# Moving the Mamba layer's x branch from the second phase of a four-layer kernel to the first, with its end states by DMA and two of sixteen states scaled by diagonals

## The chip, the cores and the metric

The kernel runs on one core of one Trainium2 chip. The metric is the device time of one execution in microseconds. The kernel before takes 10303.82 us, the median of 3 runs (10300.73 to 10316.85).

## The reference, cut to what matters

Eight samples of 256 channels on a 32 x 32 image go through four layers: a block of attention and feed-forward, a second attention block, a quantized convolution block, and a Mamba layer that scans the image in four orders (rows, rows backwards, columns, columns backwards). The change concerns the last:

```python
def _selective_scan(u, dt, A, Bm, Cm):
    def step(h, inp):
        u_t, dt_t, B_t, C_t = inp
        dA = jnp.exp(dt_t[:, :, None] * A)
        h = h * dA + dt_t[:, :, None] * B_t[:, None, :] * u_t[:, :, None]
        y = jnp.einsum('bdn,bn->bd', h, C_t)
        return (h, y)
...
def _mamba(u, W_in, conv_w, conv_b, W_x, W_dt, b_dt, A_log, D, W_out):
    xz = u @ W_in.T
    x, z = jnp.split(xz, 2, axis=-1)
    xc = x.swapaxes(1, 2)
    xc = jax.lax.conv_general_dilated(xc, conv_w[:, None, :], (1,), [(D_CONV - 1, 0)], feature_group_count=D_INNER) + conv_b[None, :, None]
    x = jax.nn.silu(xc).swapaxes(1, 2)
    x_dbl = x @ W_x.T
    dt = jax.nn.softplus(x_dbl[..., :DT_RANK] @ W_dt.T + b_dt)
    Bm = x_dbl[..., DT_RANK:DT_RANK + D_STATE]
    Cm = x_dbl[..., DT_RANK + D_STATE:]
    A = -jnp.exp(A_log)
    y = _selective_scan(x, dt, A, Bm, Cm) + x * D
    y = y * jax.nn.silu(z)
    return y @ W_out.T
```

There are 512 inner channels (4 chunks of 128 partitions), 16 states, and 1024 tokens in a sequence. The four orders of a sample share the projection x; the convolution over 4 tokens looks back in its own direction, so it differs for each.

## The kernel before, in words

Every operation is first described as an object (`_Op`, L113) with an estimated cost and the 512-column blocks that it reads and writes. Strands (Python generators) yield such operations. A planner (`_Order`, L171) always emits the strand's operation that could start first by its estimates, ties by rank; what it emits is the fixed program order of each engine, and the SP queue too is issued in that order. Since all operations leave through one helper (L136), nearly every row of the profile has line L136, and rows are told apart by tile names. Buffers come from rooms (`_Room`): a strand that takes from an empty room waits until another has put a buffer back.

**Phase A** (`phase_a`, L265) does layers 0 to 2 for all eight samples, some three of them in flight. Attention goes over TensorE (scores and values in tile `bank`), VectorE (maxima, `stats`) and ScalarE (exponentials, `exps`). Depthwise taps use ScalarE and GpSimd (`outer_taps`, L669) or VectorE (`feed_forward`, L784). Where the planner foresees a gap on TensorE it puts filler products (`fill`, L1059; their row has L1081). `layer2` (L994) ends by writing 8-bit codes to DRAM twice, as they are and turned to column order by a GpSimd copy (`codes[b][0]`, `codes[b][1]`). `weight_parts` (L1108) splits W_in into three bf16 parts and keeps them in DRAM (`w_in`). Weights stay in SBUF from the start.

**Phase B** (`phase_b`, L1142) does the Mamba layer as 64 blocks: 8 samples x 2 token orders (`swap`) x 2 directions (`back`) x 2 halves of 512 tokens. Each block has 16 groups, one for each state. What a block needs is prepared one or two blocks ahead by strands that `ahead` (L1592) starts at fixed groups:

- `inputs` (L1242): for each sample and order, x from codes and `w_in` by six bf16 products for each of 4 chunks x 2 halves, evicted by VectorE into `xi`.
- `mixed` (L1267): `conv` makes three of the four taps as fp32 products with diagonals `cvd` on TensorE and the fourth by VectorE into `xs`; `xdbl` projects `xs` to `xd`, stores the C rows to DRAM (`c_d`) and transposes B to `bT`.
- `steps` (L1315): dt from `xd` (`dt`), dt times x on GpSimd (`tmp`), transposed on TensorE and copied by VectorE to `du`, tokens on partitions.
- `tables` (L1356): one batch on ScalarE of silu of `xs` (and of the gate `z` in a quarter of the blocks) and softplus of `dt`, then back to the table with exp and ln: three table loads.

Then a group s runs over four engines. `scales` (L1453): ScalarE multiplies the four token tiles of `du` by B's column s, 128x512 each, into `dbu`. `turns` (L1463): TensorE transposes these, 16 of 128x128, into `db` in PSUM. `decays` (L1481): ScalarE makes exp(dt A) for each chunk, `da`. `scans` (L1500): VectorE's scan over `da` and `db` for each chunk, two chunks to a pair `h`. `ends` (L1522): in a block that is the first half of its direction, a ScalarE copy keeps each pair's last column in `st`, the start value for the other half. `products` (L1534): GpSimd multiplies the pair in place by C's row, which SP spreads from DRAM to all partitions (`rows`, L1493, `cb`). `sums` (L1543): TensorE transposes and adds the pair into four accumulators `py`; at group 1 x times D is added; at the end the four `py` go to `yT`, and `fold` and `outputs` finish.

The rooms that set how far an engine may run ahead are 5 `da`, 12 `dbu`, 3 `db` banks, 6 pairs `h`, 3 `cb`.

Of the kernel before, what the change touches and what calls it, by code (L numbers as in the profile page):

```python
# [42 lines left out]
TH = HALF // P  # L43
PAD = 3
# [30 lines left out]
def tile_conv_seq(ctx: ExitStack, tc: tile.TileContext, i: dict, out: bass.AP):  # L75
# [7 lines left out]
    def col(name, k=0, n=1):  # L83
# [6 lines left out]
    codes = [  # L90
        [dram.tile([CC, P, N], BF16, name=f"codes{b}_{k}", tag=f"codes{b}_{k}") for k in range(2)] for b in range(B)
# [4 lines left out]
    phase_a(tc, i, col, ident, codes, parts)  # L96
    phase_b(tc, i, col, ident, codes, parts, out)


class _Op:  # L100


    def __init__(self, engine, method, args, kw):
# [12 lines left out]
        elif engine == "vector":  # L116
            fast = near and method in ("tensor_scalar", "tensor_copy")
            both = near and method == "tensor_tensor"
            scan = method == "tensor_tensor_scan"
            self.cost = 0.04 + n * (2.2 if scan else 0.57 if fast else 1.1) + (0.3 if fast or both else 0)  # L120
        elif engine == "scalar":
            self.cost = 0.05 + 0.87 * n + (0.13 if len(ins) > 1 else 0)
        elif engine == "gpsimd":
            self.cost = 0.17 + 2.17 * n if method == "tensor_tensor" else 0.3 + n
        else:
            self.cost, self.landing = 0.1, 3.0

    @staticmethod
    def blocks(a):
        step = max(1, a.ap[0][0])  # L130
        lo = a.offset % step
        hi = lo + sum((n - 1) * abs(s) for s, n in list(a.ap)[1:])
        return [(a.name, k) for k in range(lo // 512, hi // 512 + 1)]
# [131 lines left out]
def phase_a(ctx, tc, i, col, ident, codes, w_parts):  # L265
# [19 lines left out]
    NBIG, NMID, NLOW = 12, 9, 7  # L285
# [7 lines left out]
    exps = _Room(rooms, "exps", 4, [P, 2, HALF])  # L293
    stats = _Room(rooms, "stats", 3, [P, 2, 2, NT, 4])
    bank = _Room(banks, "bank", 8, [P, HALF])
    take, takes, put = order.take, order.takes, order.put

# [3 lines left out]
    w_pi = ldk("w_pi", CC, 2 * HID)  # L301
# [3 lines left out]
    w_qkv1 = ldk("w_qkv1", CC, 3 * C)  # L305
# [478 lines left out]
    def feed_forward(b, x):  # L784
# [10 lines left out]
        at, ready, active, finished = [0], [0], [0], [0]  # L795

        def chunk(o):
            yield lambda: at[0] == o and active[0] < 2
            active[0] += 1
            at[0] += 1  # L800
            hx = yield from take(mid)
            for h in range(2):
                ps = yield from side()
                yield mm(ps, w_pi, o * P, (o + 1) * P, xn, h)
                yield A.copy(hx[:, hs(h)], ps)
                back(ps)
            acc = yield from take(mid)
# [92 lines left out]
    def layer1(b, x):  # L900
# [7 lines left out]
        ready = [0, 0]  # L908
        for cc in range(CC):
            for n, dst in enumerate((q, k)):  # L910
                for h in range(2):
                    ps = yield from side()
                    yield mm(ps, w_qkv1, n * C + cc * P, n * C + (cc + 1) * P, xn, h)
# [4 lines left out]
                    back(ps)  # L918

# [4 lines left out]
        for cc in range(CC):  # L924
            for h in range(2):
                ps = yield from side()
                yield mm(ps, w_qkv1, 2 * C + cc * P, 2 * C + (cc + 1) * P, xn, h)
                yield A.copy(v[:, cc, hs(h)], ps)
                back(ps)
        put(big, xn)  # L930
# [63 lines left out]
    def layer2(b, x):  # L994
# [34 lines left out]
        for cc in range(CC):  # L1029
# [14 lines left out]
            turned = yield from take(low, [P, N], BF16)  # L1044
            yield G.tensor_copy(turned.rearrange("p (b a) -> p b a", a=HH), cd.rearrange("p (a b) -> p b a", b=WW))
            for k, t in enumerate((cd, turned)):
                yield S.dma_start(codes[b][k][cc], t)
                put(low, t)
# [39 lines left out]
    def sample(b):  # L1088
# [17 lines left out]
        stage[b] = 4  # L1106

    def weight_parts():  # L1108


        for m, to in enumerate(w_parts):
# [9 lines left out]
            put(low, o)  # L1121

# [19 lines left out]
def phase_b(ctx, tc, i, col, ident, codes, w_parts, out):  # L1142
# [14 lines left out]
    xi_room = _Room(rooms, "xi", DC, [P, N + 2 * PAD])  # L1157
# [5 lines left out]
    h_room = _Room(rooms, "h", 6, [P, 2, HALF])  # L1163
    cb_room = _Room(rooms, "cb", 3, [P, HALF])
    tmp_room = _Room(rooms, "tmp", 2, [P, HALF])
    z_room = _Room(rooms, "z", DC, [P, HALF])
# [25 lines left out]
    cvd = wp.tile([P, DC, 3, P], F32, name="cvd", tag="cvd")  # L1192
    for c in range(DC):
        for k in range(3):
            nc.gpsimd.tensor_scalar(cvd[:, c, k, :], ident, col("cv_w", 4 * c + k), None, ALU.mult)
# [15 lines left out]
    def load_x(b, swap, h, box):  # L1211

        xf = yield from take(xf_room)
        yield S.dma_start(xf, codes[b][swap][:, :, hs(h)].rearrange("k p n -> p k n"))
# [27 lines left out]
    def inputs(b, swap, xi):  # L1242


        def first(h, box):
            if h == 0:
                tiles = yield from takes(DC, xi_room)
                for c, t in enumerate(tiles):
                    yield G.memset(t[:, :PAD], 0.0)
                    yield G.memset(t[:, PAD + N :], 0.0)  # L1250
                    xi[c] = t
            yield from load_x(b, swap, h, box)

        def one(h, c, box):
            room, ps = yield from project(box, c * P)
            yield V.tensor_scalar(xi[c][:, PAD + h * HALF : PAD + (h + 1) * HALF], ps, col("s3"), None, ALU.mult)
            put(room, ps)
            xi["done"] = xi.get("done", 0) + 1

        for h in range(2):  # L1260
            box = []
            yield first(h, box)
            for c in range(DC):
                yield one(h, c, box)


    def mixed(n):  # L1267

        d, h = blocks[n]
        xi, xd = xis[d.b, d.swap], xds[n % 2]  # L1270
        done = d.done[h]

        def conv(c):
            yield lambda: xi.get("done", 0) == 2 * DC
            t = yield from take(xs_room)
            room, ps = yield from lend()
            for k in range(3):
                o = PAD + h * HALF + (PAD - k if d.back else k - PAD)
                yield T.matmul(
                    ps, lhsT=cvd[:, c, k, :], rhs=xi[c][:, o : o + HALF], start=(k == 0), stop=(k == 2)  # L1280
                )
            o = PAD + h * HALF
            yield V.scalar_tensor_tensor(t, xi[c][:, o : o + HALF], col("cv_w", 4 * c + 3), ps, ALU.mult, ALU.add)
            put(room, ps)
            d.xs[c, h] = t
            done.add(c)
            xi["used"] = xi.get("used", 0) + 1
            if xi["used"] == 4 * DC:
                for k in range(DC):
                    put(xi_room, xi[k])  # L1290

        def xdbl():
            yield lambda: "silu" in done and (n < 2 or "dt" in blocks[n - 2][0].done[blocks[n - 2][1]])
# [19 lines left out]
        return [conv(c) for c in range(DC)] + [xdbl()]  # L1313

    def steps(n):  # L1315
# [6 lines left out]
        def dt(c):  # L1322
# [12 lines left out]
            yield lambda: "soft" in done  # L1335
# [16 lines left out]
    xis = {(b, swap): {} for b in range(B) for swap in (False, True)}  # L1352
# [3 lines left out]
    def tables(n=None, m=None, z=None):  # L1356


        def ready():
            return (  # L1360
                (n is None or len([c for c in range(DC) if c in blocks[n][0].done[blocks[n][1]]]) == DC)
                and (m is None or len(raw[m]) == DC)
                and (z is None or len(gates[z]) == DC)
            )
# [3 lines left out]
        if n is not None:  # L1368
            d, h = blocks[n]
            ops += [A.activation(d.xs[c, h], d.xs[c, h], AF.Silu, bias=col("cv_b", c)) for c in range(DC)]  # L1370
# [385 lines left out]
```

## Time and profile before

| what | us |
|---|---|
| median of 3 runs | 10303.82 |
| the profiled execution | 10303.42 |
| its span | 10301.6 |
| busy: PE / ACT / DVE / POOL | 9415.7 / 8514.4 / 7759.3 / 6131.8 |
| last `codes` store (end of phase A) | 3693 |
| first scan / last scan | 3764 / 10266 |

The page's second part shows the two phases: forty slices of the span, each digit the busy share in tenths.

```profile
PE   9989989999999989989898999899989999989988
PEld 3333323333333347777776777777777777777676
DVE  6367467575667458888887888888888888888788
ACT  7867677867666759988898998989898889899888
POOL 1433032242121048878787787778787778787778
```

The first fourteen slices are phase A, with TensorE nearly full and GpSimd little used; the rest is phase B, with all four engines at 7 to 9 tenths. The costliest rows of the groups read: line, engine, operation, written from read, count, then busy time and mean ns of one, then idle time of the engine just before, and what ended most of it.

```profile
L136 POOL TENSOR_TENSOR h<-h,cb 128x1024 f32<-128x1024 f32 x2048 | 4813.3, 2373 | 1039.1 <-DVE h L136 367.0
L136 ACT ACTIVATE da<-dt,am 128x512 f32<-128x512 f32 x4096 | 2872.0, 714 | 543.2 <-DVE h L136 537.6
L136 ACT ACTIVATE dbu<-du,bT 128x512 f32<-128x512 f32 x4096 | 2798.1, 710 | 15.4 <-PE db L136 13.6
L136 DVE TENSOR_TENSOR_SCAN h<-da,db 128x512 f32<-128x512 f32 x2048 | 2338.9, 1202 | 460.2 <-ACT da L136 131.9
L136 DVE TENSOR_TENSOR_SCAN h<-da,st,db 128x512 f32<-128x512 f32 x2048 | 2465.9, 1262 | 258.8 <-ACT da L136 139.3
L136 PE MATMUL pp<-xi,cvd 128*128 128x512 f32 x1488 | 687.8, 598 | 1.6 <-DVE ys L136 1.6
```

A group's busy time overlaps that of its neighbours, so the parts of an engine add up to more than the engine's busy time; an fp32 product counts as two records, a transpose as one.

### The profile page before, as it was taken

The page shows a single profiled execution, that of the slowest core. Times are in us where ns is not written, and L with a number is a line of the kernel's source. Part 1 is how long each engine was busy: PE and PEld are TensorE (multiplying, and loading weights), DVE is VectorE, ACT ScalarE, POOL GpSimd, SP SyncE. Part 2 cuts the span into 40 slices and gives each one's busy share as a digit, 9 for nine tenths or more (in the row PEclk, how much of TensorE's full clock was granted, in tenths as well). Part 3 has the DMA queues.
Part 4 walks back from the last instruction along what each step waited for, and adds up shares of the span by engine and source line. Part 5 has one row for each costly group of instructions (what it writes and reads, how often), then busy time and mean ns, then how long its engine had stood idle before and what let it go on. Part 6 is the DMA issues. An engine that isn't in the chain of part 4 may idle for free.

```text
span 10301.6 us, 149772 instructions
## 1 busy us (share of the span) xinstructions
PE 9415.7 (91%) x55378; PEld 5953.1 (58%) x55499; DVE 7759.3 (75%) x8675; ACT 8514.4 (83%) x15869; POOL 6131.8 (60%) x2988
## 2 busy tenths in 40 slices
PE   9989989999999989989898999899989999989988
PEld 3333323333333347777776777777777777777676
DVE  6367467575667458888887888888888888888788
ACT  7867677867666759988898998989898889899888
POOL 1433032242121048878787787778787778787778
PEclk7988989989888899999999999999999999999999
DMA  2000000000000011112111112111111111111111
GB/s 58 30 19 17 21 21 19 17 26 17 13 17 9 17 34 51 53 44 59 46 52 53 46 52 59 43 52 56 49 51 48 56 50 49 55 52 46 57 43 52
DMA packets 219616, 415.83 MB, mean 40 GB/s; under 512 B 25137, under 2 KB 67505, under 8 KB 213762
## 3 DMA queue, kind: packets, MB, share of 16 engines
q1 hardware_dynamic: 218882, 406.24, 13.1%
q8 instruction: 437, 7.16, 0.3%
q14 instruction: 297, 2.43, 0.1%
HBM read 358.43 MB, written 37.22 MB: 38 GB/s over the span
## 4 chain that ended last, share of the span: by engine, by line
PE 28%; ACT 22%; DVE 8%; issue 3%; POOL 1%; DMA 1%; DVEq 0%; SPq 0%; POOLq 0%; ACTq 0%
PE pp L136 11%; PE py L136 9%; ACT da L136 9%; PE db L136 8%; ACT dbu L136 8%; DVE h L136 7%; ACT L136 2%; ACT xs L136 1%; ACT dt L136 1%; POOL h L136 1%; ACT L145 1%; DMA wi<-w_in 1%; DVE ys L136 1%; ACT st L136 0%; ACT z L136 0%
## 5 line engine op out<-in xcount | busy, mean ns | idle before, releaser
L136 POOL TENSOR_TENSOR h<-h,cb 128x1024 f32<-128x1024 f32 x2048 | 4813.3, 2373 | 1039.1 <-DVE h L136 367.0
L136 ACT ACTIVATE da<-dt,am 128x512 f32<-128x512 f32 x4096 | 2872.0, 714 | 543.2 <-DVE h L136 537.6
L136 ACT ACTIVATE dbu<-du,bT 128x512 f32<-128x512 f32 x4096 | 2798.1, 710 | 15.4 <-PE db L136 13.6
L136 PE MATMUL db<-ident,dbu 128*128 128x128 f32 x16384 | 2385.7, 280 | 362.2 <-DVE h L136 322.6
L136 DVE TENSOR_TENSOR_SCAN h<-da,db 128x512 f32<-128x512 f32 x2048 | 2338.9, 1202 | 460.2 <-ACT da L136 131.9
L136 DVE TENSOR_TENSOR_SCAN h<-da,st,db 128x512 f32<-128x512 f32 x2048 | 2465.9, 1262 | 258.8 <-ACT da L136 139.3
L136 PEld LDWEIGHTS db<-ident,dbu 128*128 128x128 f32 x16384 | 1885.2, 143 | 875.4 <-DVE h L136 539.6
L136 PE MATMUL py<-ident,h 128*128 128x128 f32 x16384 | 2141.8, 278 | 92.4 <-POOL h L136 75.5
L136 PEld LDWEIGHTS py<-ident,h 128*128 128x128 f32 x16384 | 1878.3, 143 | 227.0 <-POOL h L136 144.2
L136 DVE TENSOR_REDUCE stats<-bank 128x1 f32<-128x512 f32 x1536 | 983.4, 684 | 545.1 <-PE bank L136 544.0
L136 ACT ACTIVATE bank<-bank,stats 128x512 f32<-128x512 f32 x1536 | 1024.9, 672 | 432.1 <-DVE stats L136 424.5
L136 PE MATMUL bank<-big,big 32*128 32x512 f32 x4096 | 987.3, 713 | 37.9 <-ACT bank L136 27.7
L136 POOL TENSOR_TENSOR mid<-mid,mid 128x961 f32<-128x961 f32 (+2 forms) x192 | 397.2, 2076 | 992.9 <-ACT mid L136 663.6
L136 ACT ACTIVATE exps<-bank 128x512 f32<-128x512 f32 x1536 | 796.5, 620 | 165.9 <-PE bank L136 156.6
L136 PE MATMUL pp<-xi,cvd 128*128 128x512 f32 x1488 | 687.8, 598 | 1.6 <-DVE ys L136 1.6
L136 PEld LDWEIGHTS bank<-big,big 32*128 32x128 f32 x4096 | 334.7, 204 | 523.7 <-issue 219.7
L136 DVE SCALAR_TENSOR_TENSOR mid<-mid,cols,mid 128x961 f32<-128x961 f32 (+1 forms) x384 | 601.6, 1567 | 6.3
L136 PE MATMUL bank<-exps,big 128*32 128x512 f32 (+1 forms) x3072 | 547.9, 621 | 3.7 <-ACT exps L136 3.7
L136 PE MATMUL bank<-big 32*128 32x512 f32 x2048 | 517.4, 724 | 32.1 <-ACT bank L136 21.5
L136 POOL TENSOR_TENSOR tmp<-dt,xs 128x512 f32<-128x512 f32 x256 | 320.9, 1273 | 322.0 <-ACT dt L136 224.4
L136 POOL TENSOR_SCALAR big<-big,ga,gs 128x512 f32<-128x512 f32 x64 | 67.7, 1070 | 712.3 <-DVE gs L136 385.5
L136 POOL TENSOR_TENSOR big<-big,mid 128x961 f32<-128x961 f32 (+1 forms) x128 | 315.2, 2472 | 270.7 <-ACT mid L136 268.6
(204 smaller groups left out, 9116.4 us busy)
## 6 DMA issues: line engine op xcount, KB each, us to landing
cb<-c_d SPq DMA_DIRECT2D x1024, 256.0 KB, 3.3
wi<-w_in SPq DMA_DIRECT2D x192, 192.0 KB, 3.5
big<-in_x_dram SPq DMA_DIRECT2D x16, 1024.0 KB, 5.0
kept<-big SPq DMA_DIRECT2D x16, 1024.0 KB, 4.5
big<-kept SPq DMA_DIRECT2D x16, 1024.0 KB, 4.8
xf<-codes SPq DMA_DIRECT2D x48, 256.0 KB, 3.8
big<-big SPq DMA_DIRECT2D x16, 512.0 KB, 6.5
codes<-low SPq DMA_DIRECT2D x32, 256.0 KB, 2.0
```

The costliest lines, as they stand in the source:

```text
L136: return getattr(getattr(nc, self.engine), self.method)(*self.args, **self.kw)
L145: nc.scalar.preload_act_table_set("natural_log_exp_and_others")
```

## The change

**The x branch moves to phase A.** After a sample's `layer2`, a strand `mix` projects x for each chunk from the stored codes, turns it to column order by a GpSimd copy, and for each order and direction makes the convolution with taps on VectorE, ScalarE and GpSimd, then silu for both directions at once between two table loads, and stores the 128x1024 result to DRAM (`mixes`). One sample is mixed at a time, one chunk at a time, in three buffers of their own; the last sample takes two chunks at a time and the `mid` buffers. The turned codes are no longer made. To make room, `w_pi` and `w_qkv1` are loaded in slices where they are used, and `mid` has 8 buffers for 9. Phase B loads `xs` from `mixes`; `inputs`, `conv`, `cvd` and the silu of `xs` go.

**End states by DMA.** `ends` issues a DMA on SP from the pair's last column (128 partitions x 2 elements of 4 bytes) into a tile of its own for each state.

**Two states by diagonals.** For states 5 and 12 of each block VectorE multiplies the identity by B's column for the four token tiles (`diagonals`), and `turns` makes `db` as fp32 products of `du` with these; `scales` leaves the two states out.

**Order.** `h` has 9 pairs for 6. The `tables` batch starts at group 4 (before: 6), `xdbl` at 8 (before: 9), the four `tmp` products at groups 5, 7, 9 and 11. The emptying of `py` is a strand of its own (`moved`). The planner has other estimates for three-operand VectorE and for GpSimd operations, and follows small tiles by 64 columns.

```diff
+ONCE = (5, 12)
+SOFT, LATER, XD = 4, (5, 7, 9, 11), 8
...
+            three = near and method == "scalar_tensor_tensor"
+            self.cost = 0.04 + n * (2.2 if scan else 1.45 if three else 0.57 if fast else 1.1) + (0.3 if fast or both else 0)
...
-            self.cost = 0.17 + 2.17 * n if method == "tensor_tensor" else 0.3 + n
+            self.cost = 0.17 + 2.17 * n if method == "tensor_tensor" else 0.1 + 2.0 * n
...
-    NBIG, NMID, NLOW = 12, 9, 7
+    NBIG, NMID, NLOW = 12, 8, 7
...
+    mx_room = _Room(rooms, "mx", 3, [P, N])
...
+    wr = _Room(rooms, "wr", 4, [P, CC, P])
...
-            turned = yield from take(low, [P, N], BF16)
-            yield G.tensor_copy(turned.rearrange("p (b a) -> p b a", a=HH), cd.rearrange("p (a b) -> p b a", b=WW))
-            for k, t in enumerate((cd, turned)):
-                yield S.dma_start(codes[b][k][cc], t)
-                put(low, t)
+            yield S.dma_start(codes[b][cc], cd)
+            put(low, cd)
...
+        order.add(RANK(b), mix(b))
...
+    def mix(b):
...
+        def branch(c, k, src, back, left):
+            o = yield from take(mx)
...
+            yield G.tensor_scalar(o, src, col("cv_w", 4 * c + PAD), col("cv_b", c), ALU.mult, ALU.add)
+            for tap in range(PAD):
+                w = col("cv_w", 4 * c + tap)
+                to, x = span(o, PAD - tap)
+                if tap < 2 or last and back:
+                    yield V.scalar_tensor_tensor(to, x, w, to, ALU.mult, ALU.add)
+                else:
+                    t = yield from take(mid)
+                    p, _ = span(t, PAD - tap)
+                    yield A.activation(p, x, AF.Identity, scale=w)
+                    yield G.tensor_tensor(to, to, p, ALU.add)
+                    put(mid, t)
+            left[back] = o
+
+        def both(c, k, src):
+            left = {}
+            for back in (False, True):
+                order.add(RANK(b), branch(c, k, src, back, left))
+            yield lambda: len(left) == 2
+            ops = [A.activation(o, o, AF.Silu) for o in left.values()]
+            yield (2.56 + sum(o.cost for o in ops), ops + [_Table()])
+            for back, o in left.items():
+                yield S.dma_start(mixes[b][k][back][c], o)
+                put(mx, o)
+
+        def chunk(c):
+            yield lambda: c in made and active[0] < two_at_once
+            active[0] += 1
+            w = yield from take(low, [P, CC, 3, P], BF16)
+            yield S.dma_start(w, w_parts[c])
+            xi = yield from take(mx)
+            for h in range(2):
+                xc = yield from take(low, [P, CC, HALF], BF16)
+                yield S.dma_start(xc, codes[b][:, :, hs(h)].rearrange("k p n -> p k n"))
+                ps = yield from side()
...
+                yield V.tensor_scalar(xi[:, hs(h)], ps, col("s3"), None, ALU.mult)
+                back(ps)
...
+            yield from both(c, 0, xi)
+            xp = yield from take(mx)
+            yield G.tensor_copy(xp.rearrange("p (b a) -> p b a", a=HH), xi.rearrange("p (a b) -> p b a", b=WW))
+            put(mx, xi)
+            yield from both(c, 1, xp)
...
+        last = b == B - 1
+        yield lambda: last or not mixing
+        mixing.append(b)
+        active, left, two_at_once = [0], [DC], 1 + last
+        mx = mid if last else mx_room
...
-    h_room = _Room(rooms, "h", 6, [P, 2, HALF])
+    h_room = _Room(rooms, "h", 9, [P, 2, HALF])
...
+    dg_room = _Room(rooms, "dg", 1, [P, TH, P])
...
+        def load():
+            tiles = yield from takes(DC, xs_room)
+            for c, t in enumerate(tiles):
+                yield S.dma_start(t, mixes[d.b][d.swap][d.back][c, :, hs(h)])
+                d.xs[c, h] = t
+            done.add("x")
...
-            yield lambda: "soft" in done
+            yield lambda: "soft" in done and place[0] >= DS * (n - 1) + LATER[c]
...
+    def diagonals():
+        for g, (n, d, h, s) in enumerate(groups):
+            if s in ONCE:
+                yield lambda: "bT" in d.done[h] and place[0] >= g - 3
+                o = yield from take(dg_room)
+                b = d.bT[:, h * TH : (h + 1) * TH, s : s + 1]
+                yield V.tensor_tensor(
+                    o, ident.unsqueeze(1).to_broadcast([P, TH, P]), b.to_broadcast([P, TH, P]), ALU.mult
+                )
+                dgs[g] = o
...
+                        T.matmul(
+                            ps[:, t * P : (t + 1) * P], lhsT=d.duT[h][:, t, c * P : (c + 1) * P], rhs=dgs[g][:, t],
+                            start=True, stop=True,
+                        )
...
-                    o = d.st.rearrange("p (c s) -> p c s", s=DS)[:, c : c + 2, s : s + 1]
-                    yield A.copy(o, pair[:, :, e : e + 1])
+                    o = d.st[s][:, c : c + 2].unsqueeze(2)
+                    yield S.dma_start(o, pair[:, :, e : e + 1])
...
-                jobs += zip((1, 2, 3, 5, 9), mixed(k))
+                jobs += zip((1, XD), mixed(k))
             if m is not None:
-                jobs.append((6, tables(k, m, z)))
-            if n % 4 == 1 and n + 3 < len(blocks):
-                e = blocks[n + 3][0]
-                jobs += zip((8, 8, 9, 10, 11, 11, 12, 13, 14, 15), inputs(e.b, e.swap, xis[e.b, e.swap]))
+                jobs.append((SOFT, tables(m, z)))
```

## The prediction

> **What bounds the kernel now.** I read the busy time by stretches first, because the kernel has two phases with different limits. The columns are: length, then busy time and count on PE, PEld, DVE, ACT, POOL, then granted clock, DMA share, GB/s.
>
> ```profile
> 1210.00:3690.00 2480.00, 2331.83 (x10407) 846.78 (x10405) 1558.84 (x2284) 1745.10 (x3830) 567.97 (x294) 0.90 0.05 18
> 3690.00:3764.00 74.00, 50.10 (x144) 20.69 (x146) 19.34 (x28) 21.68 (x30) 18.92 (x34) 0.85 0.18 56
> ...
> 4635.00:9500.00 4865.00, 4409.42 (x30073) 3469.61 (x30165) 4117.29 (x3997) 4367.06 (x7533) 3875.34 (x1855) 0.97 0.17 52
> ```
>
> The first row is phase A once sample 0 is through: PE is busy 94% (194 us of it filler products, L1081), ACT 70%, DVE 63%, POOL 23%. The second is the passage to phase B, from the last `codes` store to the first scan. The third is phase B at its steady pace. It holds 3048 scans, 64 to a block, so 47.6 blocks of 102.1 us. Per block PE is busy 92.6, ACT 91.7, DVE 86.5, POOL 81.4 us: four engines near their limit, none at it. From first scan (3764) to last (10267) it is 64 blocks of 101.6 us.
>
> Then the waits of DVE in that third stretch (total us, times, longest), because DVE has the scans, which no other engine can take:
>
> ```profile
> DVE h L136 <- ACT da L136: 209.0, 50, 7.4
> DVE xs L136 <- PE pp L136: 136.8, 77, 3.0
> DVE h L136 <- PE py L136: 127.1, 163, 4.9
> DVE h L136 <- PE db L136: 95.8, 66, 2.5
> DVE h L136 <- ACT dbu L136: 45.3, 24, 4.9
> DVE h L136 <- POOL ys L136: 33.9, 5, 7.1
> ```
>
> DVE idles 748 us there, 15.7 us a block: for decays and scaled inputs from ACT, for the convolution from PE, for a free `h` pair. Where ACT is late is seen in its timeline at a table change:
>
> ```profile
> 7061.58 1.28 ACT L136 ACT_TABLE_LOAD   x1
> 7062.88 2.57 ACT L136 ACTIVATE xs<-xs,cols 128x512 f32<-128x512 f32 x4
> 7065.35 2.17 ACT L136 ACTIVATE z<-z 128x512 f32<-128x512 f32 x4
> 7067.53 1.28 ACT L136 ACT_TABLE_LOAD   x1
> 7068.82 2.19 ACT L136 ACTIVATE dt<-dt 128x512 f32<-128x512 f32 x4
> 7071.03 1.28 ACT L145 ACT_TABLE_LOAD   x1
> ```
>
> For 10.7 us ACT makes no decay; five `da` buffers last about 6 us.
>
> **What the Trainium skill says.** ScalarE: Activation LUTs, "What ACT_TABLE_LOAD costs": 1283 ns and a drain, 2.66 us for a switch. Here the load takes 1.28 us and the next activation starts 1.30 us after it, so I use 1.29. VectorE: DVE Perf Modes, "Mode 2×_2P": an fp32 tensor_tensor stays at one element a cycle; with the 150 cycles of start in "Side-by-side", 512 elements are an estimated 0.69 us. The nearest rows here give 0.69 (`yT<-py,yT`) and 0.87 us (`big<-big,cols,low`). DMA: Bandwidth & Descriptors, "Anatomy of one DMA": some 2.0 us fixed, mostly the write receipt. The trace has 1.6 us for `c_d<-xd` and 2.3 us for `low<-in_w_in`, which has 256 pieces.
>
> **Phase B, a block.**
> ACT: 8 of 64 `dbu` go (0.613 us from start to start in the timeline: 4.9), 16 end-state copies on average (0.09 each: 1.4), 4 silu (2.6), a table load in most blocks (0.9). 91.7 − 9.8 = 81.9.
> PE: 24 records of `pp<-xi,cvd` at 0.43 us (six take 2.58 in the chain) are 10.3, 12 bf16 products of the x projection at 0.22 are 2.6. Added: two states take real fp32 products of two records each, 0.118 us a record (eight `py<-dd,xs` start to next 0.94), for transposes at 0.109: 32 × (0.235 − 0.109) = 4.0. 92.6 − 8.9 = 83.7.
> DVE: four convolution sums and two `xi` evictions at 0.65 start to start, −3.9; two diagonals at 0.8 (0.69 to 0.87), +1.6. 86.5 − 2.3 = 84.2.
> POOL: 81.4, less two memsets. Nothing else leaves it.
> SP: the 2/3 of `wi` and `xf` loads that served x go, four `xs` loads come, two blocks ahead; half of the blocks issue 32 end-state DMAs, at 0.35 us of SP each.
>
> Now the waits of DVE. Those for the convolution (2.9 a block) go. Those for ACT (`da`, `dbu`, `xd`: 280, or 5.9 a block) shrink to a third, 2.0: the table pause becomes two loads and four softplus, 4.8 us, which five `da` tiles cover. Those for PE py, a free pair (2.7), halve with nine pairs for six. POOL ys (0.7) goes, because LATER spreads the `tmp` products over groups 5 to 11. PE db and the small evictions (3.5) stay, since the diagonal states make PE's part longer. That leaves 6.8. I add 1.0 for what comes late next: POOL, at 81 of some 92, with a `tmp` now between its `h` products. 84.2 + 6.8 + 1.0 = **92.0 us**, from 102.1: −10.1 × 64 = **−646 us**. Bounds: 87.5 (all but 3 us of waits gone), −934; and 97 (half of the saved waits return at other engines), −326.
>
> The end-state DMA adds a wait: POOL's product overwrites the pair that the DMA reads, so it starts about 2.3 us after the scan's end, not at the ACT copy (POOL waited 248 us for those, 5.2 a block). It delays, but the DMAs overlap each other. POOL's rate isn't touched while DVE runs ahead in nine pairs: I take zero, between −1 and +3 us a block. `moved` as a strand of its own, the separate `st` tiles and the finer planner bookkeeping: zero, within the same bounds.
>
> **Phase A.** A sample adds, for 4 chunks × 2 orders × 2 directions: on DVE 32 taps at 1.6 us (rows of 961 and 992 elements: 1.57) and 8 evictions at 0.73, 57 us; on POOL 16 scalings at 2.1 (512 elements: 1.07), 16 sums at 2.4, 4 turns at 2.0, less the 2 old turns of 1.97: 76 us; on ACT 16 taps at 1.15, 16 silu at 1.07, 16 table loads at 1.29: 56 us; on PE 48 products at 0.265: 13 us. SP gets 28 more DMAs a sample, and 14 weight loads (the `w_pi` and `w_qkv1` slices).
> Seven samples do it inside the stretch 1210–3690: ACT 1745 + 393 (86%), DVE 79%, POOL 44%, PE 89 on its 2138 without filler (90%). DVE and POOL have room, and PE's 89 us fit into the 194 of filler. ACT's don't fit free of charge: each pair of silu holds ACT for 1.29 + 2 × 1.07 + 1.29 = 4.7 us, while PE waits for exponentials, and PE is the bound. Lower bound 0 (ACT has 735 us idle there), upper bound 393 + 89 = 482 (all in series). I take 0.4 of it, **+200**.
> The last sample has no cover: its x comes when everything else is done. DVE then has 40 taps and 8 evictions, 70 us, POOL 61, and the first load and last silu and store add some 15: **+85** (60 to 120; the two old turns at the end save about 4).
> The passage: the block's first x projection and convolution (PE from 3703 to 3749) become four loads of about 4 us: **−40** (−30 to −45).
>
> **Sum.** The profiled execution took 10303.4 us (span 10301.6, 1.8 around it), the median of the runs 10303.8, so no correction is needed. 10304 − 646 + 200 + 85 − 40 = 9903; with the 4 of the turns about **9900 us**.
>
> **Rivals.**
> *Phase A hides it all.* Speaks for it: ACT, DVE and POOL idle 735, 921 and 1912 us in that stretch. Then blocks of 87.5 us, phase A +50, ends +45: 10304 − 934 + 95 = 9465. Against: PE and ACT hand each other exponentials.
> *Phase A swallows it.* All of ACT and PE in series, +482, and a tail of 120: 10304 − 646 + 482 + 120 − 40 = 10220. For it: PE is busy 94%. Against: a twelfth of that is filler.
> *SP's queue becomes the bound (slower).* Its queue mostly stands at a row of C:
>
> ```profile
> SPq L136 <- POOL h L136: 4205.8, 750, 29.8
> ```
>
> A `cb` row waits for a buffer, which POOL's product frees. An end-state DMA issued behind such a row can't start before that product ends, and the next product waits for that DMA. If this closes in each group, a group of a first-half block is two products (4.7), two issues (0.8) and a landing (2.3): 7.8 us for 5.75, so 33 us a block in 32 blocks, +1050: 10950. It decides from 38% of those groups on (404 of 1056), where the gain is gone. For it: the planner prices the DMA's read at 0.1 us, so its order knows nothing of the landing. Against: three rows are in flight, and by the planner's costs the next pair's scans are over 2.3 + 0.35 us after the last, its latency included, and the row is due 0.8 + 2.34 + 0.35 after it (wait, product, latency), so the DMA stands first.
>
> That the work is not really moved can't be: both phases are issued in a fixed order.
>
> **How the numbers follow.** My forecast has 0.56 (by its own bounds some 9740 to 10060), all hidden 0.15, swallowed 0.16, the queue 0.13. The range leaves out the queue case and the far part of the hidden one: 9580 to 10240. Faster by over 0.2%, about what a measurement can tell here, is 0.56 + 0.15 + most of the swallowed case, 0.83; within it 0.03; slower 0.14.
>
> **What the new profile would show.** First scan at about 4010; 90 to 94 us a block, DVE at 91%; no PE wait for `xs`; ACT's table pause under 5 us; phase A's stretch longer with ACT near 85%. If first-half blocks are longer than second-half ones by over 5 us and POOL waits for DMA `st`, the queue case is at work. Wrong from the start would be: a block over 97 us, or a phase A whose end moves by less than 100 or more than 480 us.

## The result and the profile after

The changed kernel takes 10322.26 us (median of 20 runs, 10303.80 to 10351.46) against 10310.33 for the kernel before on the same chips: a ratio of 1.0012, 95% interval 1.0005 to 1.0019. It is slower by a tenth of a per cent. The forecast was 9900, with a range of 9580 to 10240. The profiled execution has a span of 10320.3 us. Here are its stretches, phase A from sample 0's codes to the last codes, the passage to the first scan, and the 64 blocks (length, busy time and count on PE, PEld, DVE, ACT, POOL, clock, DMA share, GB/s).

```profile
1156.00:3985.00 2829.00, 2612.25 (x11244) 969.59 (x11273) 2053.24 (x2564) 2109.55 (x4166) 1084.13 (x531) 0.89 0.13 47
3985.00:4121.00 136.00, 63.01 (x239) 26.34 (x242) 92.68 (x61) 59.04 (x60) 83.65 (x41) 0.73 0.31 112
4121.00:10286.00 6165.00, 5330.48 (x40142) 4535.51 (x40177) 5494.81 (x5097) 5282.10 (x8280) 5218.97 (x2355) 0.98 0.22 59
```

The same three stretches of the kernel before take 2483, 71 and 6503 us. So phase A's stretch takes 346 us more and the passage 65 more, while the blocks give back 338: from 101.6 to 96.3 us each. The stretch also begins 54 us earlier, with sample 0's codes at 1156 instead of 1210. Together that is the 19 us between the two spans. The saving in the blocks is real, but half as large as forecast.

The waits of POOL in the steady stretch 4635 to 9500 (total us, times, longest) name what is new:

```profile
POOL h L143 <- DMA st<-h: 511.8, 302, 6.6
POOL h L143 <- DVE h L143: 101.4, 96, 4.9
```

The helper's line is L143 now. 512 us in 50 blocks is 10 us a block, and only half of the blocks keep end states. Measuring each block from its first scan to the first scan of the next shows it plainly: first-half blocks take 102.4 us on average (101.4 before), second-half blocks 90.3 (101.8 before). The saving stands in full in one half of the blocks, and is missing in the other.

The waits of DVE in the same stretch:

```profile
DVE h L143 <- PE db L143: 239.3, 202, 5.0
DVE du L143 <- PE pp L143: 95.7, 31, 6.3
DVE z L143 <- PE pp L143: 53.6, 20, 5.2
DVE h L143 <- ACT da L143: 48.0, 39, 3.7
```

The wait for ACT's `da` fell from 209 us to 48, and the waits for the convolution (137) and for a free pair (127) are gone, as forecast. ACT's table change answers to the 10.7 us of before:

```profile
6251.24 1.28 ACT L143 ACT_TABLE_LOAD   x1
6252.53 2.19 ACT L143 ACTIVATE dt<-dt 128x512 f32<-128x512 f32 x4
6254.74 1.28 ACT L152 ACT_TABLE_LOAD   x1
```

It now takes 4.8 us. But PE's products come late (239), because PE waits for POOL in its own order, first before and then after the change:

```profile
PE py L136 <- POOL h L136: 54.4, 86, 1.4
```

```profile
PE py L143 <- POOL h L143: 324.0, 349, 4.1
```

How POOL comes to wait is seen where SP's and POOL's timelines are laid side by side, here in the first-half block from 6614. SP:

```profile
6649.28 0.32 SPq L143 DMA_DIRECT2D cb<-c_d  x1
6649.69 1.81 SPq L143 DMA_DIRECT2D st<-h  x2
6655.29 0.33 SPq L143 DMA_DIRECT2D cb<-c_d  x1
6655.71 1.28 SPq L143 DMA_DIRECT2D st<-h  x2
```

and POOL:

```profile
6646.90 4.67 POOL L143 TENSOR_TENSOR h<-h,cb 128x1024 f32<-128x1024 f32 x2 [4.62 <-DMA st<-h]
6652.89 4.71 POOL L143 TENSOR_TENSOR h<-h,cb 128x1024 f32<-128x1024 f32 x2 [1.32 <-DMA st<-h]
6658.88 2.36 POOL L143 TENSOR_TENSOR h<-h,cb 128x1024 f32<-128x1024 f32 x1 [1.28 <-DMA st<-h]
```

At 6655.29 a C row goes out, and only behind it the two end states. That is the order in which the row waits for the very product (6652.89 + 2.4) that frees its buffer, and the next product (6658.88) waits for the DMA behind the row. Counted over the whole trace, 311 of the 1024 end-state DMAs were issued behind a row that itself went out only after the scans of their pair had ended. They came 2.6 us after the scans on average, the other 713 came 0.3 us after.

### The profile page after: what moved, and what is told of

The parts are those of the page before. It is cut to its first block, busy times and chain, and to the rows that moved or that the text cites. A ratio compares the mean times of both kernels' runs of the same rounds, so it can differ in the third digit from the quotient of the medians.

```text
span 10320.3 us, 154404 instructions
## 1 busy us (share of the span) xinstructions
PE 9132.2 (88%) x56207; PEld 5979.7 (58%) x56277; DVE 8311.8 (81%) x8745; ACT 8338.8 (81%) x14404; POOL 6742.2 (65%) x3114
## 2 busy tenths in 40 slices
DMA packets 575968, 549.65 MB, mean 53 GB/s; under 512 B 310290, under 2 KB 377234, under 8 KB 570083
## 4 chain that ended last, share of the span: by engine, by line
PE 39%; DVE 29%; ACT 10%; issue 7%; POOL 7%; DMA 7%; SPq 0%; DVEq 0%; POOLq 0%; ACTq 0%
PE bank L143 19%; DVE h L143 16%; PE db L143 7%; POOL h L143 6%; DMA st<-h 5%; PE py L143 5%; PE pp L143 5%; DVE mid L143 4%; ACT da L143 3%; DVE stats L143 3%; ACT dbu L143 2%; DVE mx L143 2%; PE bank L1104 2%; ACT bank L143 1%; ACT mid L143 1%
## 5 line engine op out<-in xcount | busy, mean ns | idle before, releaser
L143 POOL TENSOR_TENSOR h<-h,cb 128x1024 f32<-128x1024 f32 x2048 | 4841.8, 2390 | 950.6 <-DMA st<-h 639.8
L143 ACT ACTIVATE da<-dt,am 128x512 f32<-128x512 f32 x4096 | 2871.5, 713 | 698.2 <-DVE h L143 684.4
L143 DVE TENSOR_TENSOR_SCAN h<-da,db 128x512 f32<-128x512 f32 x2048 | 2354.8, 1202 | 355.9 <-PE db L143 247.5
L143 PE MATMUL py<-ident,h 128*128 128x128 f32 x16384 | 2182.6, 278 | 426.6 <-POOL h L143 421.5
L143 ACT ACTIVATE dbu<-du,bT 128x512 f32<-128x512 f32 x3584 | 2472.1, 709 | 103.6 <-PE db L143 100.1
L143 DVE TENSOR_TENSOR_SCAN h<-da,st,db 128x512 f32<-128x512 f32 x2048 | 2452.5, 1258 | 73.5 <-PE db L143 54.9
L143 PE MATMUL db<-ident,dbu 128*128 128x128 f32 x14336 | 2117.7, 280 | 200.3 <-DVE h L143 187.7
L143 PEld LDWEIGHTS py<-ident,h 128*128 128x128 f32 x16384 | 1861.4, 142 | 557.0 <-POOL h L143 540.4
L143 PEld LDWEIGHTS db<-ident,dbu 128*128 128x128 f32 x14336 | 1652.1, 143 | 565.7 <-DVE h L143 406.0
L143 DVE TENSOR_REDUCE stats<-bank 128x1 f32<-128x512 f32 x1536 | 983.1, 683 | 399.2 <-PE bank L143 397.7
L143 ACT ACTIVATE bank<-bank,stats 128x512 f32<-128x512 f32 x1536 | 1024.2, 676 | 342.7 <-DVE stats L143 335.3
L143 PE MATMUL bank<-big,big 32*128 32x512 f32 x4096 | 1034.1, 719 | 53.5 <-ACT bank L143 28.6
L143 ACT ACTIVATE exps<-bank 128x512 f32<-128x512 f32 x1536 | 795.0, 622 | 145.6 <-PE bank L143 142.7
L143 POOL TENSOR_TENSOR mid<-mid,mid 128x961 f32<-128x961 f32 (+3 forms) x200 | 437.8, 2195 | 589.6 <-ACT mid L143 393.6
L143 DVE SCALAR_TENSOR_TENSOR mid<-mid,cols,mid 128x961 f32<-128x961 f32 (+4 forms) x424 | 719.2, 1698 | 12.0 <-POOL mid L143 4.6
L143 PEld LDWEIGHTS bank<-big,big 32*128 32x128 f32 x4096 | 362.0, 206 | 545.3 <-issue 237.5
L143 PE MATMUL bank<-exps,big 128*32 128x512 f32 (+1 forms) x3072 | 552.2, 624 | 5.5 <-ACT exps L143 5.4
L143 PE MATMUL db<-dg,du 128*128 128x128 f32 x4096 | 552.2, 285 | 4.8 <-DVE h L143 3.7
L143 POOL TENSOR_TENSOR mx<-mx,mid 128x1023 f32<-128x1023 f32 x112 | 299.5, 2677 | 373.2 <-ACT mid L143 279.3
L143 PEld LDWEIGHTS db<-dg,du 128*128 128x128 f32 x4096 | 506.1, 196 | 48.3 <-DVE h L143 23.4
L143 PE MATMUL bank<-big 32*128 32x512 f32 x2048 | 506.8, 739 | 25.5 <-ACT bank L143 21.6
L1104 PE MATMUL bank<-minus 128*128 128x512 bf16 x1605 | 464.4, 428 | 51.6 <-ACT bank L143 24.9
```

Source lines behind the costliest of these rows:

```text
L143: return getattr(getattr(nc, self.engine), self.method)(*self.args, **self.kw)
L1104: nc.tensor.matmul(out, lhsT=minus[:, : out.shape[0]], rhs=rhs, start=True, stop=True)
```

## The experiments

All 14 in one table. "Stretch" is first to last sample's codes, "passage" last codes to first scan, then the mean block of each kind. Whole times are medians of timed runs, or one profiled run where marked *; the other columns are from each kernel's profiled run.

| kernel | stretch | passage | first-half block | second-half block | whole |
|---|---|---|---|---|---|
| before | 2483 | 71 | 101.4 | 101.8 | 10310 |
| after | 2829 | 136 | 102.4 | 90.3 | 10322 |
| e1_copy | 2823 | 136 | 90.1 | 90.1 | 9915 |
| e2_planned | 2826 | 136 | 92.2 | 90.0 | 9983 |
| e3_actqueue | 2818 | 136 | 95.6 | 88.9 | 10079 |
| e4_dma_alone | 2484 | 71 | 107.4 | 101.5 | 10487 |
| v1_act_diag | 2829 | 139 | 88.0 | 84.6 | 9688 |
| v2_no_diag | 2826 | 136 | 90.1 | 86.3 | 9798* |
| p3_streamed | 2415 | 72 | 101.6 | 101.7 | 10212* |
| p1_no_silu | 2763 | 134 | 91.6 | 89.5 | 9890* |
| p2_no_dve_taps | 2767 | 99 | 91.1 | 89.3 | 9831* |
| p7_project | 2451 | 81 | 91.5 | 89.1 | 9510* |
| p6c_backfill | 2686 | 336 | 88.1 | 84.6 | 9741 |
| p9_no_third | 2688 | 137 | 90.9 | 89.6 | 9796* |
| p10_both_cuts | 2674 | 100 | 90.4 | 89.4 | 9720* |
| v4_dve_taps | 2774 | 137 | 88.0 | 84.6 | 9631 |

### The end states

**e1_copy**: undo this part alone.

```diff
-                    yield S.dma_start(o, pair[:, :, e : e + 1])
+                    yield A.copy(o, pair[:, :, e : e + 1])
```

> The changed kernel with one part undone: end states are read by the ScalarE copy again (into the separate tiles), no DMA. In the changed kernel first-half blocks take 102.4 us, second-half blocks, which keep no end state, 90.3. Theory (the wait of GpSimd for the end-state DMA is what the block pace lost): first-half blocks fall to 91 to 94 us, 32 of them by some 10, so about 10320 - 320 = 10000 us. Rival (first-half blocks are long because ScalarE's work on them is the bound, and the copies come on top): stays within 1% of 10320.

9914.78 us, ratio to before 0.9617 (0.9601 to 0.9633). Both kinds of block take 90.1 us. The end-state DMA costs 12.3 us in each of 32 blocks, 393 us. In the stretch 4635 to 9500 PE's wait for POOL falls from 324 us to 19, and VectorE's for `db` from 239 to 136. The rival, that ScalarE was the bound in these blocks, falls: ScalarE got the copies back.

**e2_planned**: the same DMA on the same queue, in another order.

```diff
+                    r.hold = 3.0
...
-                    self.read.setdefault(k[0], {})[k] = (t + cost, e)
+                    self.read.setdefault(k[0], {})[k] = (t + cost + getattr(o, "hold", 0.0), e)
```

> The changed kernel, its end states still by DMA on SP; only the planner is told that the DMA reads its pair for 3 us, so that rows of C, which wait for GpSimd, are put behind the end-state DMAs that are due before them. Theory Q (an end-state DMA stands behind a row of C in SP's queue): GpSimd's wait for the DMA falls from 640 us to under 250 and the time to about 10050. Theory L (the landing of some 2.5 us itself holds the product): the wait stays over 500 us and the time within 0.7% of 10320.

9983.45 us, ratio 0.9688 (0.9668 to 0.9707). Over the whole run POOL's wait for the DMA falls from 640 us to 320, not to below 250. In the stretch 4635 to 9500 it is

```profile
POOL h L143 <- DMA st<-h: 282.2, 198, 5.5
```

against 511.8, and a third less often than 302 times. But first-half blocks fall to 92.2, and only 49 of the 1024 DMAs still go out behind such a row. So 10.2 of the 12.3 us were the planned order, and some 2.1 are left for the landing (1.8 us here, median) and the issue. That rest is little more than the spread: in the six kernels that share e1_copy's phase B (e1_copy, p1, p2, p7, p9, p10) first-half blocks take 90.1 to 91.6.

**e3_actqueue**: the DMAs from ScalarE's queue.

```diff
-                    yield S.dma_start(o, pair[:, :, e : e + 1])
+                    r = A.dma_start(o, pair[:, :, e : e + 1])
+                    r.cost, r.landing = 0.1, 3.0
```

> The changed kernel with the end-state DMAs issued from ScalarE's queue, where no row of C stands ahead of them; each still takes its landing. Theory Q: first-half blocks fall to 92 to 96 us, 10050 to 10120 in all, less than the copy gains by what the issues cost on ScalarE. Theory L: first-half blocks stay at 100 or more, 10280 or above.

10079.46 us, ratio 0.9781 (0.9748 to 0.9814), first-half blocks 95.6, as theory Q has it: away from the C rows the landing alone doesn't hold the blocks at 102. What is left above e1_copy was not taken apart; each issue holds ScalarE's queue for 0.60 us, where the copy took 0.18.

**e4_dma_alone**: the kernel before with only this part, a tile for each state included.

```diff
-                    yield A.copy(o, pair[:, :, e : e + 1])
+                    yield S.dma_start(o, pair[:, :, e : e + 1])
```

> The kernel before with one part of the change alone: end states by DMA on SP into a tile for each state; all else as before (six pairs). Theory (queue and landing delay GpSimd): first-half blocks grow from 101.4 by 10 to 20 us, the second-half blocks stay at 102, so 10630 to 10950. Rival (in the kernel before ScalarE is the bound, and losing its copies gives 1.5 us a block): 10250 to 10310.

10487.01 us, ratio 1.0176 (1.0156 to 1.0197). It is slower, as the theory says and the rival doesn't, but by less than the interval given: first-half blocks grow by 6.0 us, not by 10 to 20. 279 of its 1024 DMAs go out behind such a row, 2.1 us late on average. Why they cost half as much as in the changed kernel is not shown.

### The diagonals

The changed kernel's diagonal is priced at 0.8 us in the forecast. Its own rows (shortest, median, longest in ns), in the changed kernel and then in e1_copy:

```profile
L143 DVE TENSOR_TENSOR dg<-ident,bT x128: 661/1684/3982, 4132.7 to 10252.1; 128x512 f32<-128x512 f32 x128
```

```profile
L143 DVE TENSOR_TENSOR dg<-ident,bT x128: 655/1122/11073, 4127.2 to 9850.1; 128x512 f32<-128x512 f32 x128
```

One of them in e1_copy on VectorE, and what POOL did meanwhile:

```profile
4735.28 4.59 DVE L143 TENSOR_TENSOR dg<-ident,bT 128x512 f32<-128x512 f32 x1
```

```profile
4732.33 6.99 POOL L143 TENSOR_TENSOR h<-h,cb 128x1024 f32<-128x1024 f32 x3
```

It starts during the second of three back-to-back products and ends 0.55 us after the third (4739.32). The shortest, beside which no product ran for most of the time, took 0.66. The Trainium skill, GPSIMD Engine Reference, "Specifications", says that GpSimd shares its SBUF interface with VectorE and that VectorE instructions with two SBUF inputs contend; this trace agrees. Of the 128 diagonals, 99 took over 0.8 us, and each of these ended 0.55 us after the end of a GpSimd instruction: 55 waited for one to end, 44 for two to six. In 46 cases a GpSimd product began before the diagonal had ended. It took 2.8 us on average instead of 2.4, so GpSimd pays too. What decides which of the two goes first is not shown. The scans, with one operand in PSUM, are not held (1.20 us as before).

**v1_act_diag**: ScalarE makes the diagonals.

```diff
-                yield V.tensor_tensor(
-                    o, ident.unsqueeze(1).to_broadcast([P, TH, P]), b.to_broadcast([P, TH, P]), ALU.mult
-                )
+                for t in range(TH):
+                    yield A.activation(o[:, t], ident, AF.Identity, scale=b[:, t])
```

> e1_copy with the diagonals made by ScalarE, four activations of 128x128 with B's column as scale, in place of one VectorE operation. In e1_copy that operation takes 2.3 us on average (0.66 at the least, 11 at the most), because it stands still until GpSimd's product ends. Theory (VectorE, 95% busy there, is the bound, and these 4.6 us a block are waiting for the SBUF port): VectorE sheds 4.6 us a block, ScalarE takes 1.6, the block goes from 90.1 to 87 to 88.5, and the time from 9915 to 9740 to 9850. Rival (ScalarE, 92% busy, is as near its limit): 9880 to 9960.

9688.47 us, ratio 0.9396 (0.9379 to 0.9412), better than the interval given: the mean block falls from 90.1 to 86.3. VectorE sheds 4.5 us a block (5508 to 5222 us busy over 64). TensorE was busy 76 us less in the blocks with the same products, at a granted clock of 1.00 instead of 0.98; what share of the gain goes with that is not shown.

**v2_no_diag**: no diagonals at all.

```diff
-ONCE = (5, 12)
+ONCE = ()
```

> e1_copy without the diagonals: all 16 states scaled by ScalarE as in the kernel before. Theory (VectorE pays 4.6 us a block for them, ScalarE would pay 4.9 and is at 92%): the block stays within 1.5 us of 90.1, so the two states by diagonals as the change makes them give nothing: 9850 to 10010. Rival (they do unload ScalarE where it counts): above 10050.

9797.61 us, below the interval given. The block is 88.2, not within 1.5 of 90.1 but 1.9 less: as the change makes them, the diagonals don't give nothing, they cost 117 us. On ScalarE they gain 109 against having none.

### Phase A

**p3_streamed**: the kernel before with only the room made.

```diff
-    NBIG, NMID, NLOW = 12, 9, 7
+    NBIG, NMID, NLOW = 12, 8, 7
...
-    w_pi = ldk("w_pi", CC, 2 * HID)
-    w_qkv1 = ldk("w_qkv1", CC, 3 * C)
...
+            loaded[o] = yield from weights("w_pi", o)
```

> The kernel before with only the room made: w_pi and w_qkv1 loaded in slices where they are used, 8 mid buffers for 9; no mix, phase B as before. T3 (the room is what phase A pays for): its stretch from first to last sample's codes grows from 2483 us by 100 or more. Otherwise it stays within 50, and the whole within 60 of 10308.

10212.15 us. Making room costs nothing: the stretch is 68 us shorter than before. Why was not pursued. The mix's price in the stretch is then 2823 − 2415 = 408 us (e1_copy against this kernel). Some 27 us of it are an earlier start of the stretch: its end comes 381 us later, at 3981 instead of 3600.

**p1_no_silu** and **p2_no_dve_taps** take one suspected engine's work out.

```diff
-            ops = [A.activation(o, o, AF.Silu) for o in left.values()]
-            yield (2.56 + sum(o.cost for o in ops), ops + [_Table()])
+            ops = [A.activation(o, o, AF.Identity) for o in left.values()]
+            yield (sum(o.cost for o in ops), ops)
```

> The changed kernel with end states copied (the run e1_copy), and in the mix of phase A the silu replaced by a plain copy without its two table loads: it leaves the silu out. In e1_copy the stretch from sample 0's codes to the last sample's takes 2823 us (1158 to 3981), in the kernel before 2483. Theory T1, that of the prediction (the silu pauses on ScalarE, 56 of 4.7 us before the last sample, hold up the exponentials): the stretch falls by 100 us or more. Rival T2 (the taps on VectorE, 399 us put among the maxima): it falls by less than 40.

```diff
-                    yield V.scalar_tensor_tensor(to, x, w, to, ALU.mult, ALU.add)
+                    continue
```

> e1_copy with the mix's taps on VectorE left out (two of the four taps of each branch, three in the last sample's backward branches), so x is not the convolution. T2 (VectorE's taps are what phase A grew by): the stretch of 2823 us falls by 150 to 330. T1 (ScalarE's pauses) or T3 (making room: weights in slices, one mid buffer fewer): by less than 80. The passage from the last codes to the first scan, 136 us, falls by some 40 to 60 in any case, since the last sample's mix has 64 us of taps on VectorE.

The stretch is 2763 without the one, 2767 without the other, some 56 to 60 us less each. Both theories fall: neither ScalarE's pauses nor VectorE's taps alone hold phase A. Without the taps the passage falls too, from 136 to 99.

**p7_project** leaves only the projection, one scaling, the turn and the stores.

```diff
-            for tap in range(PAD):
...
-            ops = [A.activation(o, o, AF.Silu) for o in left.values()]
-            yield (2.56 + sum(o.cost for o in ops), ops + [_Table()])
+            yield A.activation(left[True][:, :8], left[True][:, :8], AF.Identity)
```

> e1_copy with the mix of phase A cut to its projection, the scaling by the last tap, the turn to column order and the stores: all other taps and the silu with its table loads are left out. The two single cuts (no silu; no VectorE taps) each took only 56 us from the stretch of 2823, of which making room can't be the cause (the kernel with the room alone has 2414). Theory T4 (no single engine is full; each mix operation, on whatever engine, stands in an in-order queue ahead of the attention chain, so the price is the sum): the stretch falls by 200 to 350. Rival T6 (the mix's projection, its low buffers, its banks or its DMAs hold the samples up): it falls by less than 150.

2451: 372 of the 408 us go with the element work, more than T4's 350, though every engine had room for its part. The projection, its buffers and its DMAs (T6) are not it. But this stretch ran at a granted clock of 0.94, that of e1_copy at 0.89. TensorE's products, without filler, were busy 2114 us instead of 2270, at nearly the same number (10061 and 10092). How much of the 372 is faster products and how much is shorter queues these runs don't separate; the other cuts ran at 0.90 or 0.91.

**p6c_backfill** lets others go first.

```diff
-    RANK = lambda b: (2, b)
+    RANK = lambda b: (2, b, 1)
...
-... key=lambda x: (x[0], x[1][0]))
+... key=lambda x: (x[0] + (0.4 if len(x[1][0][0]) == 3 else 0.0), x[1][0]))
```

> The run v1_act_diag with one difference in phase A's planner: a mix operation counts as starting 0.4 us later than it could, so that another strand's operation which is ready within 0.4 us goes first. T4 (mix operations stand ahead of the attention chain): the stretch to the last codes falls by 40 to 150 us, and the time below 9650. Rival (the chain's operations become ready later than that, and the mix's lateness only lengthens the tail): the same within 30 us, or longer.

The stretch falls by 143 against v1_act_diag, as it would where the mix's operations stand ahead of the samples' chain. But the passage grows by 197: the work put off waits for the end. 9741.03, 53 us worse. T4's interval for the stretch came true, and so did the rival's longer end; T4's time below 9650 did not. A stretch from which work is put off is shorter in any case, so this run alone does not show T4.

**p9_no_third** and **p10_both_cuts** ask whether one part carries it.

```diff
-                else:
+                elif last:
```

> e1_copy with the third tap of the first seven samples' mix left out: the one made by ScalarE into a mid buffer and summed by GpSimd. Cut to the projection, phase A's stretch fell from 2823 us to 2451; without silu alone it was 2763, without the VectorE taps alone 2767. Theory T7 (the third tap, with its mid buffer that feed-forward wants too and its hop over two engines, is the costliest part): the stretch falls by 130 to 260. T4 (all parts weigh alike, and it takes several cuts to shorten the chain): by 30 to 100.

```diff
+            ops = [A.activation(o, o, AF.Identity) for o in left.values()]
+            yield (sum(o.cost for o in ops), ops)
...
+                    continue
```

> e1_copy with both single cuts together: no silu with its table loads, and no taps on VectorE. T4: more than the two apart, the stretch falls by 130 to 300. T7 (the third tap): by 80 to 130, the sum of the two.

The third tap (ScalarE to a mid buffer, then GpSimd) is worth 135 us, more than twice each other part, as T7 has it. The two other cuts together give 149, more than their sum of 116, as T4 has it. Both hold a share: single cuts add up to 251 of 372. The rest shows only when several are gone, or belongs to the higher clock of p7_project.

**v4_dve_taps** moves the third tap to VectorE.

```diff
-                if tap < 2 or last and back:
+                if tap < 2 or back or not last:
```

> v1_act_diag with the third tap of the first seven samples' mix on VectorE like the other two, so that no mid buffer, ScalarE scaling or GpSimd sum is needed; VectorE gets 112 more taps of 1.6 us, 180 us. T7: the stretch of 2829 us falls by 60 or more, and the time below 9640. T4 or VectorE's load: it grows by 0 to 120, and the time lies at 9690 to 9800.

9631.30 us, ratio to before 0.9345 (0.9330 to 0.9361). The stretch falls by 55, just short of T7's 60, though VectorE does more; the time is below 9640, as T7 has it. This is the fastest kernel of the study. Its chain of waits, by engine:

```profile
ACT 38%; PE 33%; DVE 21%; issue 4%; POOL 2%; DMA 1%; SPq 0%; DVEq 0%; POOLq 0%; ACTq 0%
```

where the changed kernel had PE 39%, DVE 29%, ACT 10%, POOL 7% and DMA 7%.

## Why the prediction was wrong

The sum missed by 420 us, and its terms say where. The first scan came at 4121 instead of some 4005 (3764 + 200 + 85 − 40 − 4), which is 116 of it. The 64 blocks took 6165 us instead of 5857 (6503 − 646), which is 308.

**The end-state DMA, taken at zero: this step failed.** I wrote "POOL's rate isn't touched while DVE runs ahead in nine pairs" and bounded it at 3 us a block. e1_copy puts it at 12.3 us in each first-half block, 6.2 over all blocks, 393 us. POOL fell behind although there were nine pairs. The mechanism was on record as a rival, with its place and its price of 33 us where it closes in every group, and with the point from which it decides, 38%. Its sign was on record too, and both halves of it came: first-half blocks longer by over 5 us (12.1), and POOL waiting for `st`. 12.3 is 37% of 33: the kernel ended at the point where the gain is gone. By count the order closed at least once in 274 of the 512 groups, at some 1.4 us for each and not 2.05. I gave it 0.13.

What misled me is the argument against it, that by the planner's costs the DMA stands first. e2_planned shows that the planned order is 10.2 of the 12.3 us. The planner counted 0.1 us for the read; told 3.0, it leaves 49 late DMAs of 311. Which step of the plan puts a row first is open. Work of VectorE between the scans is not it in most cases: 268 of the 311 had no other VectorE operation between the pair before and their own. 225 of them are the second of a state's two DMAs. Both write one `st` tile, and the planner counts 3.0 us for a landing, so it puts the second 3.1 us behind the first; the argument had not counted that. A tile for each pair was not tried.

**Phase A's +200: mis-sized.** The stretch grew by 346 from a start 54 us earlier, and making room saved 68 of what the mix cost, so the mix is 408 against bounds of 0 to 482. The reasoning failed too: I named silu's pauses on ScalarE as the carrier, and p1_no_silu finds 60 us there. And PE's 89 us did not go into the filler. Of the 340 us by which e1_copy's stretch is longer than before, PE is busy with products for 132, with filler for 147 (341 instead of 194), and idle for 61. Engine loads (ScalarE 75%, VectorE 73%, POOL 38% of the stretch) didn't tell the price; each part that was cut, on whatever engine, shortened the stretch.

**The tail and the passage**, 71 + 85 − 40 − 4 = 112 forecast, were 136: near.

**Diagonals at 0.8: mis-sized.** 1.87 us each in the steady stretch (189 us for 101), 2.3 in e1_copy. Of the two rows that I took, `yT<-py,yT` reads one input from PSUM, and `big<-big,cols,low` stands in phase A, where POOL was busy for 23%.

**Right:** VectorE's waits for the convolution and for a free pair went, those for ACT fell to 1.5 us a block (75 us for `da`, `dbu` and `xd`, where I had 2.0), and the table pause fell to 4.8 us as written. Second-half blocks are 90.3 us where I had 92.0; with the end states copied all are 90.1, and e1_copy's 9915 lies beside my 9900, partly by luck: its blocks are better than I had them, its phase A worse. 31 us of the miss are my own arithmetic: I took the gain from 102.1 us a block, the pace of one stretch, where the 64 blocks have 101.6.

The change is thus a large gain given back in three places: a new wait (393), the mix's cost in phase A and the passage (346 + 65, less 54 for the earlier start), and diagonals that wait for POOL (117, from v2_no_diag, with the end states copied). Open is how the third tap costs phase A 135 us, by its mid buffer or by its hop over two engines: a buffer of its own was not tried.

## What to carry to other kernels

A DMA is as late as what stands before it in its queue, so before a small read is moved to a DMA, look at what that queue waits for; if that is released by the consumer of the DMA, the two close a ring, and the planned order decides what it costs. Work moved to engines with room is not free where a chain over in-order queues is the bound. Here the mix kept the four engines busy some 1500 us more, and the stretch grew by 340: neither the part that doesn't fit (nothing, by the loads) nor the sum is the price. Leave parts out, singly and together, to find it, and look at the granted clock before comparing. And when a large change gives nothing, split the time by kind of block: one kind with the full gain and one with none points to the part that only one of them has.

## What the hardware showed that I had not expected

- A VectorE operation with both inputs in SBUF took 4.59 us instead of 0.66 beside GpSimd products, the longest 11.07. All that took over 0.8 us ended 0.55 us after the end of a GpSimd instruction (99 of 99 in e1_copy, 106 of 106 in the changed kernel), and the GpSimd products that began before such an operation had ended took 2.8 us on average instead of 2.4.
- A DMA of 256 elements of 4 bytes takes SP 0.59 us to issue, not the 0.35 of its larger neighbours, and lands in 2.5 us (median of the changed kernel): in 2.8 where a row of C was issued less than 2 us before it, in 1.8 elsewhere. The 1024 of them are 278549 packets, 575968 in all with them and 297419 in e1_copy.
